# A GNN layer on one core: where the first four groups of edges get their node rows and their places in the window

## The chip, the cores and the metric

The kernel runs on one core of one Trainium2 chip. The metric is the device time of one execution in microseconds (us); lower is better. Times before: 2222.69, 2222.79 and 2223.63 us, median 2222.79.

## The reference

A graph of 6,250 nodes (64 features each, `x`) and 206,250 edges (64 features each), sorted by `dst`. What is computed, cut to the core:

```python
row, col = src, dst
h = relu(concat([x[col], edge_attr]) @ W1a.T + b1a)      # one row of 128 per edge
h = h @ W1b.T + b1b
agg = segment_sum(h, row) / max(counts(row), 1)          # mean over the edges of a node
z = relu(concat([x, agg]) @ W2a.T + b2a) @ W2b.T + b2b
out = layernorm(x + concat([z, x]) @ Wr.T + br)
```

All is float32. The kernel sums the rows behind the first ReLU and puts W1b behind the sum, which is linear.

## The kernel before, in words

The edges are padded to 124 groups of 1,664 (13 tiles of 128). The host puts the groups in an order with step 77, so that a group k stands for the k-th in order of work; within a group the edges stay sorted by dst, and the dst of a group lie in a window of 64 nodes (WIN) that begins at the group's first dst (`first`, at most N - 64).

**The first layer as one product.** Let y = x W1a_x + b1a be a table of one row of 128 per node. For a group, `rhs` (128 x 1664) holds the 64 edge features on its upper partitions and, on its lower 64, a one-hot column per edge: 1 where the edge's dst is the partition's node of the window. `mv` (128 x 128) holds W1a's edge half above and the 64 rows of y of the window below. A product of a tile of `rhs` with `mv` is thus the argument of the first ReLU, and ACT writes the ReLU into a row buffer `orow`. In the code: `group(g)` (L880) issues the loads of `rhs` and `mv`, `columns(g)` (L897) makes the one-hot columns on VectorE (L900), `hidden(k, parts)` (L907) does the products on TensorE (L914) and the ReLUs on ACT (L915).

**How the places and y come about, before.** dst is loaded with a group on each of 124 partitions (L703). VectorE subtracts each group's window start (L707, `rel`), and the result goes to a table `relt` in HBM (L708). From it `group` reads a group's row back, copied to 64 partitions (L888). y is made for all 49 blocks of 128 nodes from x transposed (`zT`, loaded on ACT's queue, L627 and L628): 49 products (L719; each float32 product is two passes in the records), 13 copies by ACT to `part` (L720) and four writes to the table `ytab` (L723). `group` reads the 64 rows of a window from the table (L894), at an address that SP loads from `win_i`. All of this stands in the program ahead of the first block.

**The rest of a block.** For each block of 13 tiles, VectorE finds by a scan and counts a slot for each edge: edges of one bin of 128 source nodes lie together (`bins_of` L804, `counts_of` L825 on TensorE, `slots` L837, giving `rowidx`, L855). `scatter` (L917) then issues 13 indirect DMAs on GpSimd (L921), each of 128 rows of 130 values, from `orow` to `rows` in HBM. There are five row buffers `orow` and four `rhs`. The blocks form five epochs (82, 17, 14, 7 and 4 blocks). What lies finished in `rows` is read back (`read` L965), summed per node by products with one-hot matrices (`nodes_of`, `summed`, L1017) into `part`, while the next blocks are scattered; behind the last epoch the node layers follow (`finish`, `nodes`). At blocks 2, 4, 6, 8 and on, ACT's queue clears slots in `rows` that may stay empty (`clear` L946, four parts of 4,680 KB for the first epoch).

**What sets the order.** From L1130 on the order of TensorE, ACT, VectorE and SP is that of the program. The loop over blocks (L1144) calls in turn: `group(k+3)`, the counts of k+1, ten tiles of `hidden(k)`, `columns(k+2)` and `bins_of(k+2)`, other work, sums, `slots(k+1)`, three tiles of `hidden(k)`, `scatter(k)`. Each queue is in order: an instruction that waits holds all behind it on its engine, and on SP also the loads behind it. At block 0 the rest of src is split into `hi` and `lo` (`bins(HEAD, NT)`), and two reductions check the range of `rel`.

Of the kernel before, what the change touches and what calls it, by code (L numbers as in the profile page):

```python
# [17 lines left out]
P = 128  # L18
EPS = 1e-5
GRP = 52  # L20
SUB = 4
# [428 lines left out]
WIN = 64  # L450
STEP = 77
EPOCHS = (82, 17, 14, 7, 4)
HEAD = 325
FULL = (4, 8, 12, 16, 18)
BIG = 2.0**20
# [20 lines left out]
def fast_path(  # L476
# [119 lines left out]

    base_i = const.tile([1, NGR], I32, name="base_i")
    nc.sync.dma_start(base_i, first.rearrange("(o g) -> o g", o=1))
    at_i = const.tile([NGR, 1], I32, name="at_i")
    nc.sync.dma_start(at_i, first.rearrange("(g o) -> g o", o=1))  # L600

    rt_all = ep.tile([P, READS, RD * W], F32, name="rt")
    rts = [rt_all[:, i, :].rearrange("p (t f) -> p t f", f=W) for i in range(READS)]
# [1 line left out]
    def lent(i, n):  # L605
        return rt_all.rearrange("p i f -> p (i f)")[:, i : i + n]
# [15 lines left out]
    w1x_t = const.tile([D + 1, H], F32, name="w1x_t")  # L622
    nc.scalar.dma_start(w1x_t[:D, :], w1aT[:D])
    nc.scalar.dma_start(w1x_t[D:, :], b1a.rearrange("(o p) -> o p", o=1))
    zT = const.tile([P, NB * P], F32, name="zT")
    half = NB // 2 * P
    nc.scalar.dma_start(zT[:D, :half], xT[:, :half])  # L627
    nc.scalar.dma_start(zT[:D, half:N], xT[:, half:])  # L628
    MV = 4
    mv = [const.tile([P, H], F32, name=f"mv{i}") for i in range(MV)]  # L630
    for m in mv:
        nc.scalar.dma_start(m[:D, :], w1aT[D:])

    nc.vector.memset(zT[:D, N:], 0.0)
    nc.gpsimd.memset(zT[D : D + 1, :], 1.0)
# [9 lines left out]
    nc.gpsimd.iota(part_i, pattern=[[0, 1]], base=0, channel_multiplier=1)  # L645
    part_f = const.tile([P, 1], F32, name="part_f")
    nc.vector.tensor_copy(part_f, part_i)
    for e, ep_ in enumerate(epochs):
        ep_.tot = const.tile([P, 2 * HALF], F32, name=f"tot{e}")


    win_i = const.tile([1, NGR], I32, name="win_i")
    nc.vector.tensor_scalar(win_i, base_i, float(N - WIN), None, op0=ALU.min)
    at_f = const.tile([NGR, 1], F32, name="at_f")
    nc.vector.tensor_scalar(at_f, at_i, float(N - WIN), None, op0=ALU.min)


    hi = ep.tile([P, NT], BF16, name="hi")
# [20 lines left out]
    with (  # L679
# [27 lines left out]
        nc.vector.tensor_scalar(rel, dst_i, at_f, None, op0=ALU.subtract)  # L707
        nc.sync.dma_start(relt, rel)  # L708
        out_of = const.tile([P, 2], F32, name="out_of")
        nc.vector.memset(out_of, 0.0)  # L710


        yv = ytab.rearrange("(b p) h -> p b h", p=P)
        for b0 in range(0, NB, SUB):
            n = min(SUB, NB - b0)
            ps = hp.tile([P, SUB, H], F32, name="h_ps")
            for j in range(n):
                b = b0 + j
                nc.tensor.matmul(ps[:, j, :], zT[: D + 1, b * P : (b + 1) * P], w1x_t, start=True, stop=True)  # L719
            nc.scalar.copy(part[:, b0 : b0 + n, :H], ps[:, :n, :])  # L720
            if b0 + n == NB or (b0 + n) % (4 * SUB) == 0:
                c0 = b0 // (4 * SUB) * (4 * SUB)
                nc.scalar.dma_start(yv[:, c0 : b0 + n, :], part[:, c0 : b0 + n, :H])  # L723

        nc.sync.dma_start(src_i[:, HEAD:], srcT[:, HEAD:])

# [153 lines left out]
        def group(g):  # L880

            rhs = rhss[g % EDGES]
            if g > 1:
                edges(g)

            half = NG * P // 2
            rel = rhs[D:, :].bitcast(BF16).rearrange("p (h e) -> p h e", h=2)[:, :, half:]
            s = nc.sync.dma_start(  # L888
                rel, relt[g : g + 1, :].rearrange("o (h e) -> o h e", h=2).to_broadcast([WIN, 2, half])
            )  # L890
            with tc.issue_after(s.ins):
                w = nc.sync.value_load(win_i[0:1, g : g + 1], min_val=0, max_val=N - WIN)
            m = mv[g % MV]
            nc.sync.dma_start(m[D:, :], ytab[bass.ds(w, WIN), :])  # L894
            return rhs, rel, m

        def columns(g):  # L897

            rhs, rel, _ = made[g]
            nc.vector.tensor_tensor(  # L900
                rhs[D:, :].rearrange("p (h e) -> p h e", h=2), rel,
                in_win[D:, :, None].to_broadcast([WIN, 2, NG * P // 2]), op=ALU.is_equal,
            )

        made = {}

# [230 lines left out]
        )  # L1137
        for g in range(3):
            made[g] = group(g)
        slots(0, counts_of(*bins_of(0)))  # L1140
        columns(0)
        columns(1)
        ahead = bins_of(1)
        for k, ep_ in enumerate(epoch_of):  # L1144

            if k + 3 < NGR:
                made[k + 3] = group(k + 3)
            due = len(issued) + len(marked) + len(to_issue)
# [24 lines left out]
            if k == 4:  # L1173


                wps = hp.tile([P, P], F32, name="h_ps")
                nc.tensor.matmul(wps, wn1b, w2m_t, start=True, stop=True)
                wam_t = const.tile([P, P], F32, name="wam_t")
                nc.vector.tensor_copy(wam_t, wps)
                wps = hp.tile([P, D], F32, name="h_ps")  # L1180
                nc.tensor.matmul(wps, wn2b, wrz_t, start=True, stop=True)
                wzz_t = const.tile([P, D], F32, name="wzz_t")
                nc.vector.tensor_copy(wzz_t, wps)
                nwzz_t = const.tile([P, D], F32, name="nwzz_t")
# [192 lines left out]
```

## Time and profile before

| what | us |
|---|---|
| median of three runs | 2222.79 |
| the profiled execution, its own time | 2221.4 |
| its span, first to last instruction | 2219.6 |
| first scatter starts | 66.83 |
| last scatter starts | 2103.40 |
| GpSimd busy | 1552.6 |
| HBM read, written | 220.20 MB, 151.59 MB |

The page has six parts: busy time by engine; the span in 40 equal slices, a digit per slice for the tenths of busy time; DMA queues; the chain that ended last; the costliest groups of instructions, with the idle time of the engine ahead of them and what ended it; DMA issues. Engines: PE is TensorE, PEld its weight loads, DVE VectorE, ACT ScalarE, POOL GpSimd, SP SyncE, which here issues loads. A timeline line has start, busy time, engine, source line, operation, tiles, count, and in brackets the idle time ahead of it and its releaser. A waits line has the waiting engine and line, what it waited for, the total, the times, and the longest. A windows line has the stretch, its length, the busy time of PE, PEld, DVE, ACT and POOL with the number of instructions, then the granted TensorE clock, the mean share of the 16 DMA engines that was busy, and GB/s.

### The profile page before, as it was taken

How to read it: one execution, taken by the hardware profiler on the slowest of the kernel's cores; microseconds unless marked ns; L12 is line 12 of the kernel's file. 1: busy time of each engine (PE TensorE's matmuls, PEld its weight loads, DVE VectorE, ACT ScalarE, POOL GpSimd, SP SyncE). 2: the span in 40 equal slices, each digit the busy share in tenths (PEclk: the TensorE clock that was granted, in tenths of full speed). 3: DMA queues.
4: the chain of work that ended last, by engine and by line, in shares of the span. 5: the costliest groups of instructions: out<-in, count | busy, mean ns of one | idle time of the engine just before them, and what ended most of it. 6: DMA issues, size and time to landing. Idle time of an engine off the chain costs nothing.

```text
span 2219.6 us, 25265 instructions
## 1 busy us (share of the span) xinstructions
PE 1301.9 (59%) x8327; PEld 1191.4 (54%) x8327; DVE 1184.1 (53%) x2063; ACT 308.7 (14%) x791; POOL 1552.6 (70%) x1629
## 2 busy tenths in 40 slices
PE   4556753446455455454554675766666666677476
PEld 3545543445445454454454665655665566577465
DVE  2844443444535545355445664666575575575455
ACT  1211111111111111111111111111111111110034
POOL 1677777777777777777777777777777777777700
PEclk9877666777767777677676787877877877798789
DMA  5796555645445445454455665656655556576441
GB/s 147 246 340 188 165 162 181 199 133 151 142 136 160 133 141 150 114 163 137 137 156 151 189 195 176 178 178 181 189 165 174 186 177 191 187 216 207 168 123 22
DMA packets 199202, 373.67 MB, mean 168 GB/s; under 512 B 46362, under 2 KB 114908, under 8 KB 198932
## 3 DMA queue, kind: packets, MB, share of 16 engines
q1 hardware_dynamic: 115078, 218.90, 33.3%
q0 software_dynamic: 51584, 107.40, 15.5%
q10 hardware_dynamic: 32398, 45.65, 6.3%
q8 instruction: 68, 1.11, 0.2%
q14 instruction: 74, 0.61, 0.1%
HBM read 220.20 MB, written 151.59 MB: 168 GB/s over the span
## 4 chain that ended last, share of the span: by engine, by line
DMA 38%; POOL 28%; issue 15%; DVE 8%; PE 5%; SPq 2%; ACT 2%; POOLq 0%; ACTq 0%; DVEq 0%
DMA rows<-orow,rowidx 31%; POOL rows L921 28%; DMA rt<-rows 5%; DVE oh L999 2%; PE h_ps L914 2%; DVE rhs L900 1%; DMA rhs<-relt 1%; DMA rhs<-in_edgeT 1%; PE sum_ps L1017 1%; DVE had L820 1%; ACT orow L915 1%; PE h_ps L1247 1%; PE h_ps L719 1%; DVE row L850 1%; ACT y L1269 1%
## 5 line engine op out<-in xcount | busy, mean ns | idle before, releaser
L921 POOL DMA_INDIRECT rows<-orow,rowidx x1612 | 1544.9, 958 | 551.1 <-issue 398.5
L914 PE MATMUL h_ps<-mv,rhs 128*128 128x128 f32 x3224 | 589.7, 354 | 703.2 <-ACT orow L915 698.1
L914 PEld LDWEIGHTS h_ps<-mv,rhs 128*128 128x128 f32 x3224 | 565.6, 266 | 739.6 <-ACT orow L915 718.5
L1017 PE MATMUL sum_ps<-rt,oh 128*128 128x129 f32 x4006 | 497.2, 282 | 55.3 <-DVE part L1075 43.4
L1017 PEld LDWEIGHTS sum_ps<-rt,oh 128*128 128x128 f32 x4006 | 481.9, 198 | 58.6 <-DVE part L1075 45.2
L999 DVE TENSOR_TENSOR oh<-ramp,rt 128x512 f32<-128x512 f32 (+3 forms) x213 | 145.4, 703 | 465.4 <-DMA rt<-rows 463.2
L900 DVE TENSOR_TENSOR rhs<-rhs,ramp 64x1664 f32<-64x1664 bf16 x124 | 234.6, 1892 | 66.9 <-DMA rhs<-relt 63.5
L915 ACT ACTIVATE orow<-h_ps 128x512 f32<-128x512 f32 x496 | 230.2, 514 | 212.2 <-PE h_ps L914 211.7
L1150 ACT CAST orow<-lo 128x13 f32<-128x13 bf16 x124 | 26.5, 214 | 1484.8 <-DMA rows<-orow,rowidx 1484.6
L820 DVE TENSOR_TENSOR_SCAN had<-ramp,bins 128x700 bf16<-128x700 bf16 x124 | 200.3, 1615 | 4.2
L999 DVE TENSOR_TENSOR oh<-ramp,node 128x512 f32<-128x512 f32 (+3 forms) x237 | 187.1, 790 | 7.3
L996 DVE SCALAR_TENSOR_TENSOR node<-unused,rt 128x4 f32<-128x4 bf16 (+3 forms) x237 | 37.8, 161 | 211.8 <-DMA rt<-rows 211.4
L833 PE MATMUL cnt_ps<-had,one_w 128*128 128x350 bf16 x248 | 116.7, 472 | 36.1 <-DVE row L850 15.1
L850 DVE TENSOR_REDUCE row<-cnt_ps 128x14 f32<-128x700 f32 x124 | 109.1, 880 | 53.9 <-PE cnt_ps L834 53.9
L834 PE MATMUL cnt_ps<-bins,before_w 128*128 128x325 bf16 x248 | 117.4, 474 | 0.0
L814 DVE TENSOR_TENSOR bins<-ramp,hi 128x650 bf16<-128x650 f32 x124 | 108.1, 872 | 0.0
L1075 DVE TENSOR_TENSOR part<-part,sum_ps 128x258 f32<-128x258 f32 (+2 forms) x166 | 76.8, 463 | 49.6 <-PE sum_ps L1017 49.5
L834 PEld LDWEIGHTS <-before_w 128*128 128x128 bf16 x248 | 35.1, 141 | 63.2 <-issue 41.2
L1118 PE MATMUL h_ps<-zT,w2x_t 65*128 65x512 f32 (+1 forms) x26 | 19.6, 847 | 46.8 <-ACT orow L915 46.8
L1123 DVE TENSOR_SCALAR zT<-h_ps 128x512 f32<-128x512 f32 (+1 forms) x13 | 8.5, 657 | 70.8 <-PE h_ps L1122 70.8
L813 DVE TENSOR_TENSOR bins<-had,ramp 128x50 bf16<-128x50 bf16 x119 | 44.0, 370 | 2.7
L833 PEld LDWEIGHTS <-one_w 128*128 128x128 bf16 x248 | 35.9, 145 | 16.2
(109 smaller groups left out, 436.0 us busy)
## 6 DMA issues: line engine op xcount, KB each, us to landing
rt<-rows SPq DMA_DIRECT2D x242, 260.0 KB
rhs<-in_edgeT SPq DMA_DIRECT2D x124, 416.0 KB
rt<-rows SPq DMA_DIRECT2D x106, 390.0 KB
rhs<-relt SPq DMA_DIRECT2D x124, 208.0 KB
rows<-orow,rowidx POOLq DMA_INDIRECT x1612
rows<-padrow ACTq DMA_DIRECT2D x4, 4680.0 KB
rows<-padrow ACTq DMA_DIRECT2D x8, 2340.0 KB
rt<-rows SPq DMA_DIRECT2D x48, 325.0 KB
```

The lines of the kernel that those rows point to most:

```text
L814: nc.vector.tensor_tensor(by_bin[:, :, 1:], ramp[:, : 2 * HALF, None].to_broadcast([P, 2 * HALF, BLK]), hi[:, None, c0 : c0 + BLK].to_broa ...
L820: nc.vector.tensor_tensor_scan(had, on, oh, 0.0, op0=ALU.mult, op1=ALU.add)
L833: nc.tensor.matmul(v, one_w, had[:, b, :], start=True, stop=False)
L834: nc.tensor.matmul(v[:, :, :BLK], before_w, oh[:, b, 1:], start=False, stop=True)
L850: nc.vector.tensor_reduce(row, v.rearrange("p i b t -> p t i b"), axis=mybir.AxisListType.XY, op=ALU.max)
L900: nc.vector.tensor_tensor(rhs[D:, :].rearrange("p (h e) -> p h e", h=2), rel, in_win[D:, :, None].to_broadcast([WIN, 2, NG * P // 2]), op= ...
L914: nc.tensor.matmul(ps[:, j, :], rhs[:, c * P : (c + 1) * P], m, start=True, stop=True)
L915: nc.scalar.activation(orow[:, k0 : k0 + n, :H], ps[:, :n, :], AF.Relu)
L921: s = nc.gpsimd.indirect_dma_start(out=ep_.rows, out_offset=bass.IndirectOffsetOnAxis(ap=rowidx[:, t : t + 1], axis=0), in_=orow[:, j, :], ...
L999: nc.vector.tensor_tensor(res[:, at_tile : at_tile + nb * n, :], ramp[:, None, :].to_broadcast([P, nb * n, P]), node[:, :, None].to_broadc ...
L1017: nc.tensor.matmul(of_bin(b), oh[:, at_tile, :], rt[:, j * n + t, : H + 1], start=t0 + t == st.lo[b] and not last, stop=t0 + t == st.hi[b] ...
L1075: nc.vector.tensor_add(to, to, g.ps[:, : g.nb, :])
```

## The change

For groups 0 to 3 (NEAR) nothing goes through the two tables. `group(g)` loads the group's dst from the input, copied to 64 partitions of `rhs`, the edges, and the window's 64 columns of x transposed into `near`. `columns(g)` compares dst with the node number of the partition (`near_f`: window start - 64 + partition). A new function `window(g)` makes the 64 rows of y of this window by one product and copies them into `mv`. The load of x transposed, of dst by groups and of the rest of src go to SP's queue behind the loads of groups 0 to 2 (`load_rest`). The places of all groups (`places_in_windows`: `rel` and the write of `relt`) are made at the end of block 0, y's rows 0 to 31 (blocks of 128 nodes) at the end of block 1 and the other 17 in block 2. Groups 4 and 5 are loaded in block 2 behind that, from the tables. The split of the rest of src and the reductions move from block 0 to block 3. The four loads of W1a's edge half become one, and GpSimd sets the row of ones in `zT` behind its other preparations.

```diff
-    at_i = const.tile([NGR, 1], I32, name="at_i")
-    nc.sync.dma_start(at_i, first.rearrange("(g o) -> g o", o=1))
+    near_i = const.tile([P, NEAR], I32, name="near_i")
+    nc.sync.dma_start(near_i, first[:NEAR].rearrange("(o g) -> o g", o=1).to_broadcast([P, NEAR]))
...
-    nc.scalar.dma_start(zT[:D, :half], xT[:, :half])
-    nc.scalar.dma_start(zT[:D, half:N], xT[:, half:])
-    MV = 4
-    mv = [const.tile([P, H], F32, name=f"mv{i}") for i in range(MV)]
-    for m in mv:
-        nc.scalar.dma_start(m[:D, :], w1aT[D:])
+    nc.scalar.dma_start(mvs[:D], w1aT[D:, None, :].to_broadcast([D, MV, H]))
...
-    nc.gpsimd.memset(zT[D : D + 1, :], 1.0)
...
+    nc.gpsimd.memset(near[: D + 1], 1.0)
...
+    nc.vector.tensor_scalar(near_f, near_i, float(N - WIN), float(-D), op0=ALU.min, op1=ALU.add)
+    nc.vector.tensor_scalar(near_f, near_f, part_f, None, op0=ALU.add)
...
         for r in orows:
             nc.gpsimd.memset(r[:, :, H], 1.0)
+        nc.gpsimd.memset(zT[D : D + 1, :], 1.0)
...
-        nc.sync.dma_start(dst_i, dst.rearrange("(g e) -> g e", e=NG * P))
-        edges(0)
-        edges(1)
-        nc.vector.tensor_scalar(rel, dst_i, at_f, None, op0=ALU.subtract)
-        nc.sync.dma_start(relt, rel)
...
+        def load_rest():
+            half = NB // 2 * P
+            nc.sync.dma_start(zT[:D, :half], xT[:, :half])
+            nc.sync.dma_start(zT[:D, half:N], xT[:, half:])
+            nc.sync.dma_start(at_i, first.rearrange("(g o) -> g o", o=1))
+            nc.sync.dma_start(dst_i, dst.rearrange("(g e) -> g e", e=NG * P))
+            nc.sync.dma_start(src_i[:, HEAD:], srcT[:, HEAD:])
+
+        def places_in_windows():
+            nc.vector.tensor_scalar(at_f, at_i, float(N - WIN), None, op0=ALU.min)
+            nc.vector.tensor_scalar(rel, dst_i, at_f, None, op0=ALU.subtract)
+            nc.sync.dma_start(relt, rel)
...
-        for b0 in range(0, NB, SUB):
...
+        def y_rows(b_lo, b_hi):
+            for b0 in range(b_lo, b_hi, SUB):
...
-        nc.sync.dma_start(src_i[:, HEAD:], srcT[:, HEAD:])
...
         def group(g):
             rhs = rhss[g % EDGES]
-            if g > 1:
+            if g < NEAR:
+                all_of = dst[g * NG * P : (g + 1) * NG * P].rearrange("(o e) -> o e", o=1)
+                s = nc.sync.dma_start(rhs[D:, :].bitcast(I32), all_of.to_broadcast([WIN, NG * P]))
                 edges(g)
+                with tc.issue_after(s.ins):
+                    w = nc.sync.value_load(win_i[0:1, g : g + 1], min_val=0, max_val=N - WIN)
+                nc.sync.dma_start(near[:D, g, :], xT[:, bass.ds(w, WIN)])
+                return rhs, None, mv[g]
+            edges(g)
...
         def columns(g):
             rhs, rel, _ = made[g]
+            if g < NEAR:
+                nc.vector.tensor_scalar(
+                    rhs[D:, :], rhs[D:, :].bitcast(I32), near_f[D:, g : g + 1], None, op0=ALU.is_equal
+                )
+                return
...
+        def window(g):
+            ps = hp.tile([P, H], F32, name="h_ps")
+            nc.tensor.matmul(ps[D:, :], near[: D + 1, g, :], w1x_t, start=True, stop=True)
+            nc.scalar.copy(mv[g][D:, :], ps[D:, :])
...
         for g in range(3):
             made[g] = group(g)
-        slots(0, counts_of(*bins_of(0)))
+        load_rest()
+        window(0)
+        counts = counts_of(*bins_of(0))
         columns(0)
-        columns(1)
-        ahead = bins_of(1)
+        slots(0, counts)
         for k, ep_ in enumerate(epoch_of):
-            if k + 3 < NGR:
+            if k + 3 < NGR and k not in (1, 2):
                 made[k + 3] = group(k + 3)
...
+            if k == 0:
+                hidden(k, ((0, 4), (4, 3), (7, 3), (10, 3)))
+                window(1)
+                columns(1)
+                ahead = bins_of(1)
             if k + 1 < NGR:
                 counts = counts_of(*ahead)
-            hidden(k, ((0, 4), (4, 3), (7, 3)))
+            if k > 0:
+                hidden(k, ((0, 4), (4, 3), (7, 3)))
+            if k + 2 < NEAR:
+                window(k + 2)
+            if k == 2:
+                y_rows(Y_AHEAD, NB)
+                made.update({g: group(g) for g in (NEAR, NEAR + 1)})
...
-            if k == 0:
+            if k == 3:
                 bins(HEAD, NT)
...
-                    hidden(k, ((10, 3),))
+                    if k > 0:
+                        hidden(k, ((10, 3),))
...
+            if k == 0:
+                places_in_windows()
+            if k == 1:
+                y_rows(0, Y_AHEAD)
```

More of the change, by code (lines that the diff above doesn't have):

```diff
@@ L452 @@
 EPOCHS = (82, 17, 14, 7, 4)
+NEAR = 4
+Y_AHEAD = 32
 HEAD = 325
@@ L624, in fast_path @@
     nc.scalar.dma_start(w1x_t[D:, :], b1a.rearrange("(o p) -> o p", o=1))
+    MV = 4
+    mvs = const.tile([P, MV, H], F32, name="mv")
+    nc.scalar.dma_start(mvs[:D], w1aT[D:, None, :].to_broadcast([D, MV, H]))
+    mv = [mvs[:, i, :] for i in range(MV)]
     zT = const.tile([P, NB * P], F32, name="zT")
-    half = NB // 2 * P
-    nc.scalar.dma_start(zT[:D, :half], xT[:, :half])
-    nc.scalar.dma_start(zT[:D, half:N], xT[:, half:])
-    MV = 4
-    mv = [const.tile([P, H], F32, name=f"mv{i}") for i in range(MV)]
-    for m in mv:
-        nc.scalar.dma_start(m[:D, :], w1aT[D:])
+    near = lent(2 * NT + NG * P * 3 // 2, NEAR * WIN).rearrange("p (g w) -> p g w", w=WIN)
     nc.vector.memset(zT[:D, N:], 0.0)
-    nc.gpsimd.memset(zT[D : D + 1, :], 1.0)
     iota_i = const.tile([P, P], I32, name="iota_i")
@@ L653, in fast_path @@
     nc.vector.tensor_scalar(win_i, base_i, float(N - WIN), None, op0=ALU.min)
-    at_f = const.tile([NGR, 1], F32, name="at_f")
-    nc.vector.tensor_scalar(at_f, at_i, float(N - WIN), None, op0=ALU.min)
+    near_f = const.tile([P, NEAR], F32, name="near_f")
+    nc.vector.tensor_scalar(near_f, near_i, float(N - WIN), float(-D), op0=ALU.min, op1=ALU.add)
+    nc.vector.tensor_scalar(near_f, near_f, part_f, None, op0=ALU.add)
     hi = ep.tile([P, NT], BF16, name="hi")
@@ L714, in fast_path @@
-        for b0 in range(0, NB, SUB):
[L715 to L723, printed above, removed]
@@ L725, in fast_path @@
-        nc.sync.dma_start(src_i[:, HEAD:], srcT[:, HEAD:])
+        at_i = const.tile([NGR, 1], I32, name="at_i")
+        at_f = const.tile([NGR, 1], F32, name="at_f")
+        def load_rest():
[5 more added lines that the diff above has]
+            nc.sync.dma_start(src_i[:, HEAD:], srcT[:, HEAD:])
@@ new lines, in places_in_windows @@
+        def places_in_windows():
+            nc.vector.tensor_scalar(at_f, at_i, float(N - WIN), None, op0=ALU.min)
+            nc.vector.tensor_scalar(rel, dst_i, at_f, None, op0=ALU.subtract)
+            nc.sync.dma_start(relt, rel)
+        yv = ytab.rearrange("(b p) h -> p b h", p=P)
+        def y_rows(b_lo, b_hi):
+            for b0 in range(b_lo, b_hi, SUB):
+                n = min(SUB, b_hi - b0)
+                ps = hp.tile([P, SUB, H], F32, name="h_ps")
+                for j in range(n):
+                    b = b0 + j
+                    nc.tensor.matmul(
+                        ps[:, j, :], zT[: D + 1, b * P : (b + 1) * P], w1x_t, start=True, stop=True
+                    )
+                nc.scalar.copy(part[:, b0 : b0 + n, :H], ps[:, :n, :])
+                if b0 + n == NB or (b0 + n) % (4 * SUB) == 0:
+                    c0 = b0 // (4 * SUB) * (4 * SUB)
+                    nc.scalar.dma_start(yv[:, c0 : b0 + n, :], part[:, c0 : b0 + n, :H])
@@ L899, in columns @@
             rhs, rel, _ = made[g]
+            if g < NEAR:
+                nc.vector.tensor_scalar(
+                    rhs[D:, :], rhs[D:, :].bitcast(I32), near_f[D:, g : g + 1], None, op0=ALU.is_equal
+                )
+                return
             nc.vector.tensor_tensor(
```

## The prediction

> **What bounds the kernel now.** First the page's busy rows, its 40 slices and its fourth part, for the engine that sets the pace.
>
> ```profile
> PE 1301.9 (59%) x8327; PEld 1191.4 (54%) x8327; DVE 1184.1 (53%) x2063; ACT 308.7 (14%) x791; POOL 1552.6 (70%) x1629
> ...
> POOL 1677777777777777777777777777777777777700
> ...
> L921 POOL DMA_INDIRECT rows<-orow,rowidx x1612 | 1544.9, 958 | 551.1 <-issue 398.5
> ```
>
> GpSimd (POOL) is the busiest, nearly all of it scatters, and its row is flat: a first slice with little, a constant middle, two empty slices. So I asked for the scatters alone (by line), then their timeline.
>
> ```profile
> L921 POOL DMA_INDIRECT rows<-orow,rowidx x1612: 952/958/1764, 66.8 to 2103.4; - x180
> ```
> ```profile
> 66.83 1.76 POOL L921 DMA_INDIRECT rows<-orow,rowidx  x1 [58.44 <-ACT orow L915]
> 68.90 1.26 POOL L921 DMA_INDIRECT rows<-orow,rowidx  x1 [0.30 <-issue]
> 70.46 0.96 POOL L921 DMA_INDIRECT rows<-orow,rowidx  x1 [0.30 <-issue]
> ...
> 84.34 0.95 POOL L921 DMA_INDIRECT rows<-orow,rowidx  x1 [0.30 <-issue]
> ```
>
> One scatter starts each 1.262 us, 13 to a block, so a block takes 16.4 us. 1,611 steps at 1.262 are 2,033 us; the measured 2,036.6 (66.8 to 2103.4) leaves 3 us of waiting in the whole run. The kernel is: 66.8 us until the first scatter, 2,036.6 us of scatters, 116.2 us of tail (to 2219.6). A change ahead of the first scatter is worth what it moves that scatter, less any new hole between scatters. The waits of the first 70 us say what holds it:
>
> ```profile
> POOL rows L921 <- ACT orow L915: 58.4, 1, 58.4
> ...
> DVE rt L707 <- DMA rt<-in_dst_o: 18.7, 1, 18.7
> ...
> DVE rhs L900 <- DMA rhs<-relt: 15.9, 2, 15.0
> ```
>
> The chain in order of time names the same: dst and the edge loads to 27.6, the y products to 47.3, the table's write to 53.2, a read of relt to 57.6, VectorE to 62.2, first products at 63.4.
>
> **Part 1: what the first scatter will wait for.** The instruction order of the changed kernel, built, shows none of dst in rows, relt, zT, ytab ahead of the first products. Left are three chains.
>
> Loads: srcT, then dst (64 copies) and edges of group 0, all on SP's queue. srcT was in use at 4.3 in before; 832 KB more at 251 GB/s (58:60 us) take 3.3 us, so they are there by about 8, its 16 KB of x at 9. Not last.
>
> VectorE: here the first timeline matters.
>
> ```profile
> 0.75 5.32 POOL L635 MEMSET zT<- 1x6272 f32 x1 [0.29 <-POOLq L1359]
> ...
> 2.01 4.13 DVE L653 TENSOR_SCALAR win_i<-base_i 1x124 int32<-1x124 int32 x1 [0.72 <-DMA base_i<-in_first]
> ...
> 3.46 2.68 DVE L655 TENSOR_SCALAR at_f<-at_i 124x1 f32<-124x1 int32 x1
> ```
>
> Two tiny operations end at 6.14, just behind the memset: VectorE stood still for it. The change puts this memset last of POOL's preparations. These took 6.15 to 8.38, plus some 0.25 for the new memset of `near` (256 elements against 6272 in 5.32), so the long one runs about 3.3 to 8.6. win_i (data at 2.0) gets through ahead of it, srcT's operations (4.3) do not. From 8.6: near_f and three operations on srcT 1.1 (as to 7.04 behind 6.07), then the row ramp to `had`, 26.72 to 30.92, 4.2: 14.0. The columns of group 0 are now one operation with a scalar operand; its nearest row is L707, 1.085 us for 1664 elements (above: 1.89 as L900): 15.1.
>
> PE and on: counts 1.15 (62.27 to 63.41) from 14.0, products at 15.2, first ReLU 1.95 later, 0.60 long, scatter 0.87 behind it: **18.6**. Bounds: 16 if the memset doesn't hold VectorE, 22 if the new columns take 1.89 as L900 and a load is late. Gain 66.8 - 18.6 = **48.2 us**.
>
> **Part 2: what is pushed in between scatters.** If none comes late, block k may start at 18.6 + 17.5 + 16.41(k-1): block 1 at 36.1, 2 at 52.5, 3 at 68.9, 4 at 85.3. The blocks must be made in this time together with y.
>
> Block 1: VectorE ends slots of block 0 at 16.4 (counts 15.2, then 1.06); two columns of 1.08 and two bins of 2.67 (81.49 to 84.17) bring it to 23.9. PE's counts of 2 to 25.1, then 3.4 to the scatter: 28.5, allowed 36.1. In time. Before, ACT waited 1,484.6 us for scatters to free its row buffers: blocks had a lead, which here must first be won.
>
> Block 2: PE's order is ten products of block 1, the window product of group 3, three products, 32 rows of y, counts, block 2. The window waits for group 3's x, behind xT and dst on SP's queue. Groups 0 to 2 are 2.54 MB at 251 GB/s, to 12.8; xT 1.6 MB, to 19.2; dst is the slow one:
>
> ```profile
> 18.00:20.00 2.00, 2.00 (x11) 2.00 (x11) 0.00 (x0) 0.00 (x0) 0.00 (x0) 1.00 0.25 80
> 20.00:22.00 2.00, 1.32 (x7) 1.03 (x5) 0.00 (x0) 0.00 (x0) 0.00 (x0) 1.00 0.26 70
> 22.00:24.00 2.00, 0.00 (x0) 0.00 (x0) 0.00 (x0) 0.00 (x0) 0.00 (x0) 1.00 0.24 71
> ```
>
> The last columns: DMA share 0.25 at 70 to 80 GB/s, so four of 16 engines still work, and the trace waits for dst in this time. 825 KB at 75 are 11 us: 30.2. The rest of srcT and group 3 queue behind it on these four: 4.5 more, scatter traffic beside: **36**. VectorE waits in the same place, in `places_in_windows` for dst (to 30) and for group 3's dst; behind it lie bins of 3, needed on PE only after y. Then three products to 37.5, and y.
>
> The 49 products of y are 98 passes; rows 16 to 48 are 20.9 us of 98 (40 in 8.55), 0.214 each. The Trainium skill, page "TensorE: Matmul & The Clock Gate", Part 1, says the clock doubles after some 3.4 us of sustained work. By that rule y would run at about the hidden products' faster pace, 26 passes in 3.06 at clock 1.00 (80.7 us), 0.118. The row speaks against it: 17 us of y without a break stayed at the pace that 26 hidden passes have at clock 0.5 (5.37 us, 0.207), though the page's clock row shows 1.00 there, ahead of its first record. I take 0.214; by the rule block 2 would be 6 us earlier. 64 passes: 51.2; counts 52.4; scatter of block 2 at 55.8, **3.3 late**.
>
> Block 3: ten products to 56.5, 17 rows of y (34 passes, 7.3) to 63.8, three products, counts to 66.3, first ReLU done 68.9, scatter 69.8; allowed 72.2 behind the first delay. In time.
>
> Block 4 is the first to need the table. y's last copy and write issue at 64.9; the write took 5.3 (47.93 to 53.24): 70.2. SP stands at the read of group 4's y rows until then, and behind it in SP's queue are all loads of groups 5 and 6. relt of group 5 goes out at 71.4. Its landing: 3.6 us undisturbed (54.02 to 57.62), 10.7 beside a clear of 4.7 MB (84.78 to 95.51). The clear of block 2 is issued by ACT right behind the table, so 10.7: 82.1. VectorE then: columns 1.89, bins 2.67, the rest of srcT 2.5 and the two reductions over dst 3.7 (both moved from block 0 to 3), slots 1.06: 93.9, against 85.3: **8.6 late**. This contains the 3.3; delays of blocks don't add, the largest counts. Bounds: 0 (y at the faster clock, 9 us less), 16 (SP's queue waiting for free semaphores, a second slow load). Block 5 needs 6 us of VectorE after that and has 16: the lead grows from there.
>
> **Part 3: two-port work beside scatters.** The Trainium skill, page "SBUF — State Buffer", section "SBUF: two separate sides" (the trap at its end), says that a VectorE operation using the shared port keeps GpSimd from writing descriptors; it speaks against this change, which puts rel and the columns of groups 2 and 3 (1.08 each) under scatters. The trace: L664 (0.81) and L666 (0.83) lay beside the first two scatters, and these took 1.76 and 1.26 for 0.96, 1.1 together, 0.55 each. By the row three operations cost **1.6 us**, by the page's full lock 3.2, nothing where they meet the 0.30 gaps. srcT's operations move with their 1.1: no change.
>
> At nothing: y's 13 copies lie on ACT, 14% busy, in step with PE (1.71 per four products against 0.58; without that cover 13 x 0.58 = 7.5 in blocks 1 and 2); the table's four writes and the one mv load are only issued there, 0.2 to 0.5 each. The ten weight loads stand behind relt on SP and are used at block 4, as before. The tail, 116 us, isn't touched.
>
> **Sum**, against the profiled execution (2221.4: span 2219.6 and 1.8 around it): 2221.4 - 48.2 + 8.6 + 1.6 = 2183.4. The median shown is 1.4 above that execution: **2185**.
>
> **Rivals.**
> B, no hole: y at the faster clock or quick loads; block 4 in time. For it: scatters never wait once under way in before. Against: the rows of y. 2221.4 - 48.2 + 1 + 1.4 = 2176.
> C, a large hole, 13 to 40 us: SP's queue stops twice (dst's four engines, then the table), so block 2 or 4 is 25 late: 2202. For it: waits of 10.5 us for relt even with a lead (118.5). Against: each group is 0.65 MB, small against 16.4 us.
> D, slower: the one place is SP's queue at the table. If clears hold groups 5 and later to more than a block's time each, the delay grows at every block till the last early clear and decides from 53 us on: 2230. Against: in before one group per 11 us came in beside clears.
> E, the start doesn't move as said, or gain and hole cancel: within 0.2%, 2223.
>
> **Chances.** A (hole 3 to 13) 53%, B 27%, C 15%, D 3%, E 2%. Faster 0.95, same 0.02, slower 0.03; 0.2% (4.4 us) is about what a measurement of this kernel tells from no change. Range: B with the first scatter at 16 and nothing for the ports or a hole is 2221.4 - 50.8 + 1.4 = 2172; C's nearer half reaches 2198.
>
> **What would show it.** First scatter at 16 to 22 us, with VectorE idle till about 8.6; gaps in the POOL row at blocks 2 and 4 of 3 and 5 us, released by ACT (block 2) and VectorE's rowidx (block 4); y at 0.21 per pass; SP's read of ytab at about 70; pace 1.262 and tail 116 as before. Wrong if the hole lies in another block, if columns take 1.9, or if the pace changes.

## The result and the profile after

| | before | after |
|---|---|---|
| median, us | 2223.21 (2222.69 to 2223.85) | 2193.89 (2192.87 to 2195.07) |
| ratio of the times, 95% interval | | 0.9868 [0.9851, 0.9885] |
| profiled execution: own time, span | 2221.4, 2219.6 | 2194.12, 2192.3 |
| first scatter starts | 66.83 | 17.71 |
| last scatter starts | 2103.40 | 2080.76 |
| behind the last scatter's start | 116.2 | 111.6 |

The changed kernel is 29.3 us faster; the forecast was 38. The same three parts of the page, and the scatters by line:

```profile
PE 1297.9 (59%) x8335; PEld 1190.7 (54%) x8335; DVE 1183.1 (54%) x2065; ACT 311.5 (14%) x795; POOL 1557.8 (71%) x1630
...
POOL 6477777777777777777777777777777777777700
...
L956 POOL DMA_INDIRECT rows<-orow,rowidx x1612 | 1550.2, 962 | 523.2 <-issue 395.4
```
```profile
L956 POOL DMA_INDIRECT rows<-orow,rowidx x1612: 956/962/1553, 17.7 to 2080.8; - x180
```

The work is the same, and so are the busy times. What is new stands in the POOL row: the first slice (55 us each) has 6 where it had 1, the second 4 where it had 6. The scatters begin earlier and then stop. The waits of GpSimd and of VectorE say for whom:

```profile
POOL rows L956 <- ACT orow L950: 27.3, 9, 13.2
POOL rows L956 <- DVE out_of L1208: 7.0, 1, 7.0
```
```profile
DVE rhs L929 <- DMA rhs<-relt: 72.8, 11, 28.2
DVE rt L724 <- DMA rt<-in_dst_o: 14.6, 1, 14.6
```

Before, GpSimd waited 58.4 us for ACT once, at the start. Now it waits 9.4 at the start, 13.2 once more and 7.0 once. VectorE still waits for dst, no longer at the head but under the scatters, and its longest wait for relt grew from 15.0 to 28.2.

The difference of the two spans, read from the starts of the scatters. A step is the time from one scatter to the next; its median is 1.263 us before and 1.266 after, and what goes beyond it is waiting.

| part of the span | before | after | difference |
|---|---|---|---|
| until the first scatter | 66.8 | 17.7 | -49.1 |
| waiting between scatters | 1.9 | 23.5 | +21.6 |
| 1,611 steps | 2034.7 | 2039.5 | +4.8 |
| behind the last scatter's start | 116.2 | 111.6 | -4.6 |
| span | 2219.6 | 2192.3 | -27.3 |

The waiting is three holes: 12.85 us ahead of block 2's first scatter, 6.65 ahead of block 3's eleventh, 2.6 ahead of block 4's first. The rest are bits of less than 1 us each.

### The profile page after: what moved, and what is told of

Same layout as the page of the kernel before. It is cut to its first block, busy times and chain, and to the rows that moved or that the text cites. A ratio compares the mean times of both kernels' runs of the same rounds, so it can differ in the third digit from the quotient of the medians.

```text
span 2192.3 us, 25272 instructions
## 1 busy us (share of the span) xinstructions
PE 1297.9 (59%) x8335; PEld 1190.7 (54%) x8335; DVE 1183.1 (54%) x2065; ACT 311.5 (14%) x795; POOL 1557.8 (71%) x1630
## 4 chain that ended last, share of the span: by engine, by line
DMA 37%; POOL 27%; issue 15%; PE 9%; DVE 7%; SPq 2%; ACT 2%; ACTq 0%; POOLq 0%; DVEq 0%
DMA rows<-orow,rowidx 28%; POOL rows L956 27%; DMA rt<-rows 5%; PE h_ps L949 3%; PE sum_ps L1052 3%; DVE oh L1034 2%; DMA rows<-padrow 1%; DMA rt<-in_xT 1%; DMA rhs<-relt 1%; DVE rhs L929 1%; ACT orow L950 1%; PE h_ps L736 1%; DVE had L837 1%; PE h_ps L1299 1%; ACT y L1321 1%
## 5 line engine op out<-in xcount | busy, mean ns | idle before, releaser
L949 PE MATMUL h_ps<-mv,rhs 128*128 128x128 f32 x3224 | 596.4, 357 | 700.7 <-ACT orow L950 700.7
L949 PEld LDWEIGHTS h_ps<-mv,rhs 128*128 128x128 f32 x3224 | 572.0, 269 | 737.9 <-ACT orow L950 721.1
L929 DVE TENSOR_TENSOR rhs<-rhs,ramp 64x1664 f32<-64x1664 bf16 x120 | 227.0, 1892 | 76.2 <-DMA rhs<-relt 72.8
L1288 ACT ACTIVATE agg<-sum_ps,rc 128x128 f32<-128x128 f32 x49 | 17.1, 365 | 118.3 <-DMA rt<-rows 90.6
```

What stands on the lines that cost most here:

```text
L929: nc.vector.tensor_tensor(rhs[D:, :].rearrange("p (h e) -> p h e", h=2), rel, in_win[D:, :, None].to_broadcast([WIN, 2, NG * P // 2]), op= ...
L949: nc.tensor.matmul(ps[:, j, :], rhs[:, c * P : (c + 1) * P], m, start=True, stop=True)
```

## The start

The timeline of the first 18 us of the kernel after:

```profile
3.01 5.32 POOL L699 MEMSET zT<- 1x6272 f32 x1
...
3.88 4.47 DVE L657 TENSOR_SCALAR near_f<-near_i 128x4 f32<-128x4 int32 x1 [0.85 <-DMA near_i<-in_first]
...
13.55 1.09 DVE L925 TENSOR_SCALAR rhs<-rhs,near_f 64x1664 f32<-64x1664 int32 x1
...
14.74 4.68 PE L949 MATMUL h_ps<-mv,rhs 128*128 128x128 f32 x26
...
16.82 0.60 ACT L950 ACTIVATE orow<-h_ps 128x512 f32<-128x512 f32 x1 [5.00 <-PE h_ps L949]
```

The memset of one partition lies at 3.01 to 8.33, and a VectorE operation on 128 x 4 elements that starts at 3.88 ends at 8.35: VectorE stands until GpSimd is done. From there the columns end at 14.64 (15.1 in the forecast), the products start at 14.74 (15.2) and the first scatter at 17.71 (18.6).

## The two late blocks

Block 2 first. In the timeline of the kernel after: SP's issue of dst, VectorE's use of it, the window product of group 3, y's first part.

```profile
14.13 0.27 SPq L719 DMA_DIRECT2D rt<-in_dst_o  x1
...
40.31 1.28 DVE L724 TENSOR_SCALAR rt<-rt,at_f 124x1664 bf16<-124x1664 int32 x1 [14.63 <-DMA rt<-in_dst_o]
...
45.41 0.66 PE L937 MATMUL h_ps<-w1x_t,rt 65*64 65x128 f32 x2 [16.30 <-DMA rt<-in_xT]
...
47.43 13.86 PE L736 MATMUL h_ps<-w1x_t,zT 65*128 65x128 f32 x64
```

TensorE stands 16.3 us in front of one small product, because group 3's x lies behind dst, and y and block 2 stand behind that product. The windows of the kernel after show the loads (last three columns: granted TensorE clock, busy share of the DMA engines, GB/s):

```profile
28.00:32.00 4.00, 1.10 (x9) 0.91 (x8) 0.00 (x0) 0.99 (x2) 3.00 (x4) 0.93 1.05 215
32.00:36.00 4.00, 0.00 (x0) 0.00 (x0) 0.00 (x0) 0.00 (x0) 2.88 (x3) 0.50 0.53 163
36.00:40.00 4.00, 0.00 (x0) 0.00 (x0) 0.00 (x0) 0.00 (x0) 3.08 (x4) 0.50 0.37 129
```

All engines are busy until 32; then the share falls to 0.37, with scatters in it, and dst is still not there. That dst moves on few engines is hidden until 32 by what is issued behind it. In the trace's DMA packets the last row of x transposed ends at 25.1; of the 128 rows of the rest of src 96 start at 23 to 29, and the other 32, a quarter, only at 38 to 42. So the engines that carry dst held back a quarter of each later load, group 3's too, while the rest of it passed.

Then block 4. The timeline of the kernel after, from the table's last write to block 4's first scatter:

```profile
71.27 3.30 ACTq L742 DMA_DIRECT2D ytab<-part  x1
...
78.04 0.50 SPq L918 DMA_DIRECT2D mv<-ytab  x1
...
80.09 1.44 SPq L912 DMA_DIRECT2D rhs<-relt  x1
...
91.80 1.89 DVE L929 TENSOR_TENSOR rhs<-rhs,ramp 64x1664 f32<-64x1664 bf16 x1 [28.21 <-DMA rhs<-relt]
...
98.78 3.67 DVE L1208 TENSOR_REDUCE out_of<-rt 124x1 f32<-124x1664 bf16 x2
98.90 1.26 ACT L670 CAST lo<-rt 128x1287 bf16<-128x1287 int32 x1 [20.95 <-DVE rt L669]
100.07 0.48 ACT L950 ACTIVATE orow<-h_ps 128x384 f32<-128x384 f32 x1
...
100.83 0.96 POOL L956 DMA_INDIRECT rows<-orow,rowidx  x1 [6.96 <-DVE out_of L1208]
...
103.28 0.17 DVE L872 SCALAR_TENSOR_TENSOR rowidx<-row,bin_at 128x13 int32<-128x13 f32 x1
103.29 0.45 PE L850 MATMUL cnt_ps<-had,one_w 128*128 128x350 bf16 x1 [24.59 <-DVE bad L1354]
...
104.41 3.50 PE L949 MATMUL h_ps<-mv,rhs 128*128 128x128 f32 x20
...
107.24 0.96 POOL L956 DMA_INDIRECT rows<-orow,rowidx  x1 [2.92 <-ACT orow L950]
```

Two things are to be seen. The scatter at 100.83 is put down to VectorE's reduction, but the bracket names only the releaser that came last by the profile. ACT's ReLU of 0.48 us at 100.07 is what it needs, and that stands on ACT behind the cast of `lo`, which waited 20.95 us for the src split on VectorE; VectorE itself had waited 28.2 us for relt. And block 4's first products wait for more than their own data: TensorE has the counts of block 5 ahead of them, these wait until `slots` of block 4 have read the counts before them (24.59 us), and so the products of block 4 follow at 104.41 and its scatter at 107.24, 3.8 us behind the end of `slots`.

## The theory and its rivals

Theory: the start is worth what it moved, 49 us; y, begun late because group 3's x lies behind dst, makes block 2 late by 12.8; relt of group 5, read only behind the table and beside a clear, makes block 4 late by 22.1 in all (12.85 + 6.65 + 2.6); 6.65 of this show already in block 3, whose last ReLUs stand behind the src split. The rest of the kernel pays nothing. Rivals: y's passes themselves, whoever lets them start, take too long for any order (R1); the loads moved under the scatters slow the scatters down everywhere (R2); the holes come from VectorE's extra work, the two-port operations among it (R3).

Three sets of runs were made, each beside the kernel before; ratios are to that set's own median of before. The holes are those of the profiled execution, as time beyond the step of 1.263.

### The kernel before, by itself

> The kernel before, run once more beside the others. In the changed kernel's profile one scatter starts each 1.266 us instead of 1.263, and 111.5 us lie behind the last scatter instead of 116.2. Theory: both belong to the change (more work beside the scatters, another order of reads at the end); then this run shows 1.263 and 116 again. Rival: they differ from one chip or execution to the next; then this run shows some other pair, such as 1.266 or 112, with a total within 0.2% of 2223.

Ratio 0.9999 [0.999, 1.0008], 2219.29 us against 2218.81. Step 1.263, first scatter at 66.07, tail 116.3, waiting between scatters 3.8. It gives the scale: the tail is the same as in the first execution of before, and a step of 1.263 belongs to this kernel.

### dst cut so that all DMA engines load it

```diff
-            nc.sync.dma_start(dst_i, dst.rearrange("(g e) -> g e", e=NG * P))
+            dst_g = dst.rearrange("(g e) -> g e", e=NG * P)
+            wide = NGR // 16 * 16
+            nc.sync.dma_start(dst_i[:wide], dst_g[:wide])
+            nc.sync.dma_start(dst_i[wide:], dst_g[wide:])
```

> The load of dst by groups is cut into 112 and 12 partitions, nothing else. Theory: the hole of 12.8 us ahead of block 2 is dst's load, whose 124 rows go to four engines only, with group 3's x queued behind it and TensorE's window product waiting for that. With 112 rows spread over 16 engines dst lands some 10 us earlier (about 30 instead of 40 us), y starts at about 37 instead of 47, and the hole ahead of block 2 shrinks to 4 us or less; the holes at blocks 3 and 4 shrink by what is left of the delay; the whole 8 to 12 us faster than the changed kernel, about 2183. Rival: the loads are held by the total of bytes and not by the four engines; then dst lands within 3 us of 40 and the time stays at 2191 to 2194.

2181.53 us, ratio 0.9839 [0.9822, 0.9855]. In its timeline:

```profile
31.11 1.09 DVE L727 TENSOR_SCALAR rt<-rt,at_f 124x1664 bf16<-124x1664 int32 x1 [5.25 <-DMA rt<-in_dst_o]
...
37.10 0.66 PE L940 MATMUL h_ps<-w1x_t,rt 65*64 65x128 f32 x2 [8.11 <-DMA rt<-in_xT]
```

The same bytes, as 112 and 12 rows, are there 9.2 us earlier (31.11 for 40.31), group 3's product 8.3 earlier, y at 39.13 for 47.43. The hole ahead of block 2 falls from 12.85 to 4.5, those at blocks 3 and 4 from 9.25 to 7.5: both hang on y's start. R1 would have left them.

### Group 3 ahead of dst

```diff
         def load_rest():
+            made[3] = group(3)
...
-            if k + 3 < NGR and k not in (1, 2):
+            if k + 3 < NGR and k not in (0, 1, 2):
```

> The loads of group 3 are issued ahead of dst's, behind x; dst keeps its four engines. Theory (TensorE's wait for group 3's x is what counts): the window product runs at about 31 instead of 45 us, y follows at once, and the hole ahead of block 2 goes to 0 to 3 us although dst lands later (about 43) and VectorE waits for it as before; about 2183. Rival (VectorE's wait for dst is what counts, since block 3's columns and bins stand behind it): counts of block 3 come at 50 or later, the hole stays at 8 us or more, about 2191.

2184.44 us, ratio 0.9847 [0.983, 0.9863]. Group 3's product now runs at 30.93 and y at 32.92, 14.5 us earlier, and yet a hole of 5.6 is left ahead of block 2 (and 0.9, 6.6 and 2.6 at blocks 3 and 4). The timeline shows a wait that was not expected:

```profile
49.35 0.65 SPq L620 DMA_DIRECT2D b2b_c<-in_b2b  x1
...
56.37 0.39 ACTq L743 DMA_DIRECT2D ytab<-part  x1
...
56.81 0.21 ACT L1187 CAST orow<-lo 128x13 f32<-128x13 bf16 x1 [9.40 <-DMA b2b_c<-in_b2b]
...
57.78 0.96 POOL L957 DMA_INDIRECT rows<-orow,rowidx  x1 [5.86 <-ACT orow L951]
```

ACT stood for 9.4 us until a load of a few bytes (`b2b_c`, on SP's queue behind `rel`, which waited for dst until 42.01) had landed, and it stood there to issue a write of y's table, which needs nothing of that load. In the trace's records the DMAs that SP and ACT issue take eight semaphores in turn, and ACT's second write of y has the one that `b2b_c`'s load had; it was issued only when that load had landed. So the order was right and its gain was half taken back by a wait between two queues.

### The src split and the reductions at block 6 instead of 3

```diff
-            if k == 3:
+            if k == 6:
                 bins(HEAD, NT)
```

> The split of the rest of src and the two reductions over dst move from block 3 to block 6. Theory: the hole of 6.7 us ahead of block 4 (released by the reductions) is VectorE's 6.2 us of this work ahead of block 4's slots; it goes to 0.5 or less, and the 2.6 us at its fourth scatter, which waits for a product, may stay or grow by what is won; 4 to 7 us faster than the changed kernel, about 2188. Rival: the late table holds block 4 by TensorE as well; then most of the hole comes back at the next scatters and the time stays within 2 us of 2194.

2183.70 us, ratio 0.9844 [0.9827, 0.986]. The hole ahead of block 3's eleventh scatter is gone, that of block 2 is unchanged (13.15 of idle time in both), and 2.9 is left ahead of block 4. `slots` of block 4 end 5.8 us earlier (rowidx at 97.50 for 103.28), with relt landed at 92.10 for 91.80. So the 6.2 us of VectorE work (2.5 and 3.7), which stand there ahead of `slots`, do cost; but they are the end of a chain that is late already, not a cause of their own (R3).

### The kernel after once more, and two ways to bring relt earlier

> The changed kernel once more, beside the next three. Theory: its holes are 12.8 us ahead of block 2, some 6.7 and 2.6 us at blocks 3 to 4, and its pace is what this chip gives to the kernel before as well (1.263 in the run of the kernel before; 1.266 was the chip's). The ratio to the kernel before stays within 0.985 to 0.989.

2190.64 us, ratio 0.9869 [0.9853, 0.9886], first scatter at 17.71, holes of 12.7, 6.2 and 2.6, tail 112.1, and a step of 1.263: the +4.8 us of steps in the first comparison do not come back. R2 falls with it, for these scatters lie beside the same loads.

The clears at blocks 5, 7, 9 and 11:

```diff
-        clears = {2 + 2 * i: (0, i) for i in range(CLEAR)}
+        clears = {5 + 2 * i: (0, i) for i in range(CLEAR)}
```

> The first four clears are issued at blocks 5, 7, 9, 11 instead of 2, 4, 6, 8. Theory (a clear of 4.7 MB beside group 5's loads makes the hole at block 4): relt of group 5 lands 4 us behind its issue at 80 instead of 11.7, VectorE ends at 96 instead of 104, and the 6.7 and 2.6 us at block 4 go: 6 to 9 us faster than the changed kernel; the hole of 12.8 stays. Rival (the table itself is late, so that any load behind it is): relt lands at 88 or later and the holes stay within 3 us.

2183.00 us, ratio 0.9836 [0.982, 0.9852], 7.6 below the kernel after on the same chip.

```profile
78.66 0.61 SPq L912 DMA_DIRECT2D rhs<-relt  x1
...
83.72 1.89 DVE L929 TENSOR_TENSOR rhs<-rhs,ramp 64x1664 f32<-64x1664 bf16 x1 [19.87 <-DMA rhs<-relt]
```

Group 5's relt is in use 5.1 us after its issue, against 11.7 beside the clear (80.09 to 91.80). The holes at blocks 3 and 4 shrink from 8.9 to 1.6 in all; the one ahead of block 2 stays (12.3).

relt of groups 4 and 5 read ahead of y's rows, the table's rows behind both:

```diff
+        later = []
+
+        def window_of(g, s):
+            with tc.issue_after(s.ins):
+                w = nc.sync.value_load(win_i[0:1, g : g + 1], min_val=0, max_val=N - WIN)
+            nc.sync.dma_start(mv[g % MV][D:, :], ytab[bass.ds(w, WIN), :])
...
-            with tc.issue_after(s.ins):
-                w = nc.sync.value_load(win_i[0:1, g : g + 1], min_val=0, max_val=N - WIN)
...
-            nc.sync.dma_start(m[D:, :], ytab[bass.ds(w, WIN), :])
+            if g > NEAR + 1:
+                window_of(g, s)
+            else:
+                later.append((g, s))
...
                 made.update({g: group(g) for g in (NEAR, NEAR + 1)})
+                for g, s in later:
+                    window_of(g, s)
```

> In block 2 SP issues edges and places of groups 4 and 5 ahead of both reads of the table of y; clears stay where they are. Theory (what counts is that SP stands at the read of the table with group 5's places behind it): relt of group 5 lands at about 58 instead of 92, VectorE's columns, bins, split and reductions are done by 85, block 4 is in time, 7 to 9 us faster than the changed kernel; the hole of 12.8 us ahead of block 2 stays. Rival (the clear would delay the reads of the table in the same way): TensorE waits for mv of group 4 until 90 or later, and most of the hole stays with ACT as its releaser.

2185.15 us, ratio 0.9849 [0.9833, 0.9866], 5.5 below the kernel after. The holes at blocks 3 and 4 are gone, and the 12.9 ahead of block 2 stay. The table is still awaited, by TensorE until 84.9, but block 4 has that time. The two runs say the same by different means: what made block 4 late was relt behind the table, and its landing beside a clear. They also show that the delays don't add: with block 4's chain shortened, what is left is block 2's delay alone.

### The row of ones by a DMA instead of GpSimd

```diff
-        nc.gpsimd.memset(zT[D : D + 1, :], 1.0)
+        nc.scalar.dma_start(zT[D : D + 1, :].rearrange("o (p c) -> o p c", p=P), ones[:, :NB])
```

> The row of ones in x transposed is copied by one DMA on ACT's queue from a tile of ones instead of GpSimd's memset of 5.3 us. Theory (VectorE stood still for this memset, from 3.0 to 8.3 us, ahead of the first scatter): srcT's operations run from about 4.5, the first scatter starts at 14 to 15.5 instead of 17.7, held then by group 0's window product, which waited for its x until 10.6. The hole ahead of block 2 grows by the same, since it hangs on the loads, so that the total gains nothing to 1 us. Rival (VectorE waited for srcT's load and not for the memset): the first scatter stays at 17.7.

2194.10 us, ratio 0.9888 [0.9871, 0.9904]: no gain. VectorE's first operation on srcT runs at 5.07 and takes 0.33, and the columns of group 0 run 3.1 us earlier (10.42 for 13.55), so GpSimd's memset is what held VectorE. But the first scatter comes only 1.0 earlier, at 16.67: now group 0's window product waits for its loads until 11.72, the counts follow it, and the products start at 13.46. The expectation had named this second limit, but at 10.6: these 1.1 us are what 16.67 lies above its 15.5. The profiled executions differ by 0.6 us (2192.41 and 2191.77), the medians by 3.5, which the traces don't explain.

### All of it together

Three builds on one chip: dst cut and group 3 ahead of it (the first two edits); with these, relt ahead of the table, the split at block 6 and the ten small weight loads at block 0 instead of 1 (`if k == 1:` to `if k == 0:`); and with all this the later clears and another division of y's rows (`Y_AHEAD = 16`: 16 blocks of nodes in block 1 and 33 in block 2).

> Both changes to the loads: dst on 112 and 12 partitions, and group 3 ahead of it. Theory (the hole ahead of block 2 is the sum of TensorE's late window product and, in the run with group 3 ahead, of ACT standing at its second write of y for a load that SP issues behind rel): dst lands at about 34, rel and the small loads go out by 42, ACT does not stand, y ends at 46, and the hole is 0 to 2 us instead of 12.8 (5.6 and 4.5 with one of them). The holes at blocks 3 and 4 stay 5 to 9 us. Some 2180. Rival (y's own 14 us on TensorE don't fit between blocks 1 and 2): a hole of 4 us or more stays.

> c1 and: places of groups 4 and 5 ahead of the reads of the table, the split of src and the reductions at block 6, the ten weight loads at block 0 ahead of the write of relt. Theory: no hole above 2 us is left before block 8, first scatter 17.7, so the changed kernel less its holes of 12.8, 6.7 and 2.6: 2168 to 2171, ratio to the kernel before 0.976 to 0.979. Rival (loads that are moved only bring another wait late, as in the run with group 3 ahead): a hole of 4 us or more at blocks 2 to 6, 2174 or above.

> c2 with the first clears at blocks 5, 7, 9, 11 and 16 rows of y in block 1, 33 in block 2. Theory: if c2 has no hole, this has none to take away either, and stays within 2 us of c2; if c2 keeps a hole at block 2 that waits for y's products, 16 rows less there (7 us) close it. Rival: the table is written 7 us later in block 2, so block 4 comes late by some us: slower than c2.

| kernel | median, us | ratio to before | waiting between scatters |
|---|---|---|---|
| first two edits | 2178.55 | 0.9821 [0.9804, 0.9837] | 9.9 |
| all but clears and y's division | 2174.99 | 0.9811 [0.9791, 0.9831] | 7.5 |
| all | 2172.47 | 0.9793 [0.9776, 0.9809] | 3.3 |

The first two edits together leave no hole ahead of block 2, and three of 1.7 to 2.6 at blocks 3 and 4. But here y's first 64 passes ran at granted clock 1.00, in 7.31 us instead of 13.86, so this build alone doesn't show that the order of the loads is enough. And ACT stood again at its second write of y, 4.9 us until 44.83, now for the load of `wn1b`; the expectation had said that it would not stand.

The second build missed its expectation by some 4 us: it has no hole above 1.7, but some ten of 0.4 to 1.7. Its y took 13.86 us again for the first 64 passes, and block 2 was in time: R1 falls, since what counts is when y starts (33.4 here, 47.4 in the kernel after).

The third is the fastest kernel of this study: its waiting is what the kernel before has (3.8), so its start at 17.7 counts in full. Its y ran at clock 1.00 (32 passes in 3.74 us, 66 in 7.54), so what the later clears and the other division are worth beside the second build is not shown apart from that. Its profiled execution is 52.8 us below the one above of the kernel before (2169.85 and 2222.67): the first scatter lies 48.4 us earlier (17.7 and 66.07), the tail is 3.9 shorter, the waiting 0.5. The medians differ by 46.7; of these two executions one was the shortest of its four, the other the longest of its twelve.

## Why the prediction was right or wrong

**The start** was right: 49.1 us for 48.2, with VectorE held until 8.35 (8.6 in the forecast) by the memset. That this is the cause is shown by the run with the DMA in its place.

**Two-port work beside scatters**: the sum was right, 1.4 us for 1.6. Three scatters are late by 0.4 to 0.6 where VectorE's operations on windows lie (20.4, 41.1 and 44.0 us). The last of them in the kernel after:

```profile
43.62 1.09 DVE L925 TENSOR_SCALAR rhs<-rhs,near_f 64x1664 f32<-64x1664 int32 x1 [2.03 <-DMA rhs<-in_dst_o]
...
43.98 1.55 POOL L956 DMA_INDIRECT rows<-orow,rowidx  x1 [0.30 <-issue]
```

Each of the three began while the operation ran, and took longer than 0.96 by what was left of the operation less some 0.13: 0.43 with 0.55 left, 0.38 with 0.52, 0.59 with 0.72. So the scatter was held to about the operation's end, and the rows agree with the lock that the Trainium skill's page "SBUF — State Buffer", section "SBUF: two separate sides", describes. The forecast's 3.2 for a full lock was too much, since it took the whole of each operation, and not what is left of it when the scatter is due. VectorE's operation of 1.89 us on `rhs` and `ramp` at 91.80 held neither scatter beside it (0.96 each).

**The hole was 22.1 where 8.6 stood**, and the case given 53%, a hole of 3 to 13, did not come. The forecast had two late blocks, 2 and 4, for the two chains that did come late; their sizes were off. But by its own sign ("Wrong if the hole lies in another block") it was also wrong for 6.65 us, which lie ahead of block 3's eleventh scatter. ACT's last ReLUs of block 3 stood there behind the cast of `lo`. The forecast had the src split only as VectorE's work ahead of block 4's `slots`, and not what ACT does behind it; with the split at block 6 this hole was gone. Of the sum three terms failed, and one erred to the other side:

- *"825 KB at 75 are 11 us: 30.2 ... 36."* dst was in use at 40.3 and group 3's product ran at 45.4. The forecast let groups 0 to 2 and x pass at 251 GB/s to 19.2; x ended at 25.1, for the stretches of 4 us from 8 to 24 moved 185 to 239 GB/s, and from 17.7 on a scatter of 66.6 KB each 1.266 us takes 53 GB/s of it. From there dst took another 15 us, for 11: the 75 GB/s had been read in the kernel before at 18 to 24 us, where no scatter ran. This term is worth 9.4 us at block 2, whose delay was thereby 12.85 for 3.3. Cutting dst alone takes 9.2 us off its landing.
- *"y's last copy and write issue at 64.9 ... 70.2 ... 82.1."* y's start was 9.9 late for the same reason. Its end was 6.3 late, the write took 7 for 5.3, and relt landed 11.7 behind its issue for 10.7, so that it came at 91.8: 9.7 late in all.
- *"slots 1.06: 93.9, against 85.3."* This set the end of `slots` against the time at which the scatter was due. The counts of block 5, which wait for these slots, and the first products of block 4 stand between them, 3.8 us. The wait of TensorE for `slots` was not seen; the last releaser at block 4 was therefore ACT, and not VectorE's `rowidx` as forecast. With 9.7 and 3.8 the forecast's 93.9 becomes 107.4; the scatter started at 107.24.
- *"34 passes, 7.3."* They took 3.96, for the clock was at 1.00 there. The 64 passes before them took 13.86, for 13.7.

That of several delays the largest counts was right: with block 4's chain mended, block 2's 12.3 or 12.9 remained, and with block 2's hole down to 4.5 by cutting dst, 12.0 remained in all at block 4. Both chains had the late y in front of them, and so one error of 9.4 us went into the larger delay nearly in full. The forecast gave a hole of 13 to 40 a chance of 15%, and its cause ("SP's queue stops twice") was what happened; the argument against it, "each group is 0.65 MB, small against 16.4 us", looked at bytes and not at how many engines carry them.

**Pace and tail** were to stay. The step was 1.266 for 1.263 in the first execution, +4.8 us, and 1.263 again in the next one of the same kernel, so that it belongs to the chip or the execution. (The forecast's 1.262 is 1.263 by the median of the starts; the kernel before then waits 1.9 us in all, not 3.) The tail was 4.6 shorter. That came back in every run of the changed kernels (111.2 to 114.5, against 116.2 and 116.3), and it stays open. In the first comparison the two cancelled (+4.8 and -4.6), and neither was forecast: that is luck. The order of the last instructions is the same, and the granted clock falls at other moments in the tail (0.91 and 1.00 in its second and third 20 us after, 0.87 and 0.96 before); that it is a matter of when the clock's slow stretches fall is only argued, not shown.

## What to carry to other kernels

When the head of a kernel is cut away by moving its work under a running pipeline, the work must still be done by a date: write down for each block when its scatter is due, and follow each chain through every queue to that scatter, to the last instruction. A load that uses few DMA engines costs its full time where something small that is needed at once is queued behind it, as group 3's 16 KB of x were. And once the start is moved, look for what stands ahead of the first block that is late, not at the sum of busy times: here reshaping one load took the ratio to before from 0.9868 to 0.9839, and reordering small things around it took it to 0.9793.

## What the runs showed of the hardware that was not expected

**The clock under y's products.** The windows of the kernel after, in y's first and second part, and of the build with the first two edits, in y's first part:

```profile
48.00:54.00 6.00, 6.00 (x30) 6.00 (x29) 0.36 (x2) 1.93 (x4) 2.94 (x4) 0.50 0.50 131
...
66.00:70.00 4.00, 4.00 (x38) 4.00 (x38) 0.00 (x0) 2.31 (x5) 2.92 (x4) 1.00 0.30 93
```
```profile
32.00:36.00 4.00, 4.00 (x38) 4.00 (x38) 1.87 (x2) 2.43 (x5) 3.21 (x3) 1.00 0.75 242
```

The same products, without a gap, at 0.217 us a pass for 13.86 us at clock 0.50, or at 0.114 (64 passes in 7.31) where they began at 1.00. In none of the runs that began at 0.50 did these 13.9 us of work raise the clock; in the second part of the build with the first two edits, which began at 1.00, it fell to 0.50 some 2 us in. Where the first part ran at 0.50, the clock rose 1.6 to 4.7 us behind its last pass, while the counts and the products of `rhs` and `mv` (128 rows, where y has 65) ran. The rule that the prediction weighed, some 3.4 us of sustained work (the Trainium skill, page "TensorE: Matmul & The Clock Gate", Part 1), is not seen for them. Whether it is the rows in use that made the difference the runs don't show.

**A load of 124 rows.** dst as one load of 124 rows kept few engines busy (0.25 in before, at 71 GB/s); as 112 and 12 rows the same bytes came 9.2 us earlier.

**A wait between two queues.** ACT stood 9.4 us for a load of SP's queue that it has nothing to do with, because the DMAs of both take the same eight semaphores in turn.

**GpSimd's memset.** One partition of 6,272 elements takes 5.32 us, and the first of VectorE's operations on loaded data that began beside it ended just behind it (8.35 for 8.33 in the kernel after, 6.14 for 6.07 before); on 128 x 4 elements that is 4.47 us for 0.17 in the run without the memset. VectorE's own memsets did not stand: six of 0.06 to 0.17 us ran beside it at 0.82 to 1.28 in the kernel before.
